# A four-layer convolution stack on one Trainium2 core: parts of g loaded three units ahead, and layer 1's last quarter spread over a longer stretch

## The chip, the cores and the metric

The kernel runs on one core of one Trainium2 chip. The metric is the device time of one execution in microseconds (us), as the median of several runs; lower is better. TensorE (PE) does the matmuls, VectorE (DVE), ScalarE (ACT) and GpSimd (POOL) do elementwise work, and SyncE's queue (SP) issues most of the DMA transfers. All five run their own queues of instructions and meet through semaphores.

## The reference

The input is `x` of shape (1024, 16, 16, 16), float32: 1024 images of 16 rows, 16 columns and 16 channels. Four layers are applied, each on a group norm of its input and with a residual:

```
def _gn(v, G=8, eps=1e-5):     # mean and variance of each image and group of 2 channels
    g = v.reshape(B_, H_, W_, G, C_ // G)
    return ((g - mean(g)) / sqrt(var(g) + eps)).reshape(v.shape)

x = x + L0(_gn(x), core0, core1, core2)          # a matrix of 4096 x 4096 in tensor-train form, ranks 1,16,16,1
x = x + L1(_gn(x), conv1, conv2, fc0, fc1)       # a step of a neural cellular automaton
x = x + L2(_gn(x), filters, bias)                # a 3x3 convolution over the image
x = x + L3(_gn(x), conv1, conv2, fc0, fc1)       # as L1, with its own weights
```

A step of the automaton (L1, L3) takes two depthwise 3x3 convolutions of its input, joins them with the input to 48 channels, applies `relu(flat @ fc0_w.T + fc0_b)` with 128 hidden values and `@ fc1_w.T + fc1_b`, adds the result `d` to its input, and sets to zero each place where the 3x3 maximum of channel 3 is not over 0.1, in the input or in `d`. Its reshapes read the channel axis as a place, so that the rows of the dense part come from all of an image; the kernel folds the convolutions into the weights of fc0.

## The kernel before

**Tiling.** The images are worked on in two half batches of 512, X0 and X1. Each stands in one large SBUF tile (`xn`, 128 partitions, 32 lines of 512 images). A line of a partition is one value of the 4096 of each image. The engines' queues are written out by the kernel itself: instructions stand on each engine in the order in which the Python code issues them.

**Layer 0.** The tensor-train matrix is multiplied in five phases, with products in the manner of Strassen (`PRODUCTS`), so that phases have 2, 7, 7, 7 and 7 products. Each phase has 16 *units* (a quarter `q` and a `w`), 80 in all. A unit needs its weights `w` (128 x 128 blocks), which are built on the chip: `gload(u)` (L1076) loads four parts of `g`, 32 KB each, from DRAM into a tile `gq`; `build(u)` multiplies them with the core `R` (`pw`, L1095, 16 matmuls in the first phase), and ScalarE copies the result to `w` (L1100). The parts of `g` are themselves products of the cores: `early` and `gs` multiply them (`pg`, L554), ScalarE copies them (L557), and `send` or `gs` store them to `g_dram` (L563, 512 KB each). A unit's matmuls `po` are at L1172. `pieces` issues them in steps of two: at the first step it builds the next unit's weights, at the second it stores the unit before (L1151 in the first phase), and in the middle of the unit (`at == mid`) it issues a later `gload`. In the first phase, TensorE also transposes the second half batch's input (`ptin`, L902), whose loads are issued on GpSimd's queue (L884).

**Layer 1.** `layer_nca` works in *quads*: four groups of rows of the hidden layer, each of several matmuls `ph` (L1562) into one of six PSUM banks (`h`), a ScalarE `Relu` to `hid` (L1565), and then L1398 into one of two banks `o`. Two quads make one step `w2`, and eight steps one quarter `q` of the output. In the first quarter the masks are made as well: at each step VectorE takes flags from the input (L1428) and from the result (L1406), adds bias and input (L1410), and some slots later TensorE counts the flags of the neighbours (`pcnt`, L1437, two of the `h` banks), from which VectorE makes the mask (L1442, L1443). GpSimd multiplies and adds (L1449, L1450), and SyncE stores.

**Work beside the matmuls.** `run(layer, us, loads, *spans)` places background work between the steps of a layer. Each span is a list of steps with costs and two fractions of the layer, for its begin and its end; a step is issued once the layer has passed its fraction. So the fractions set where in each engine's queue a background instruction stands, and no time is looked at when the kernel runs. Layer 1 on X0 begins before the group norm of X0 is complete: its last quarter of lines (24 to 31) is summed, centred and squared in the background (`last`: L614, L622, L655, L754, `pvar` L789), then come the root (L695), the Newton step (`newton`, L701 to L705: a reciprocal and four more), a spread over the partitions (`pr`, L801) with ScalarE's copy (L678), and four multiplications of two lines each (L655). The second quarter of the layer's steps is the first that reads these lines (`ph` with `wq`). The group norm of the other half batch, `norm_cw(X1)`, follows in the same manner.

Of the kernel before, what the change touches and what calls it, by code (L numbers as in the profile page):

```python
# [103 lines left out]
def conv_preact_kernel(ctx: ExitStack, tc: tile.TileContext, a: dict, out: bass.AP):  # L104
# [11 lines left out]
    xf = [  # L116
        [dram.tile([8, 4, P, NB], F32, tag=f"xf{l}_{n}", name=f"xf{l}_{n}") for n in range(NCH)]
        for l in range(5)
    ]
# [7 lines left out]
    def stage(es, sb, ps):  # L127

        for key, sizes, kw in (("sb", sb, {}), ("ps", ps, {"space": PSUM})):
            p = es.enter_context(  # L130
                tc.tile_pool(name=f"{key}{len(pool)}", bufs=1, reuse_waits="tile", **kw)
            )
            pool[key] = p, sizes
        pool[len(pool)] = None

    def work(shape, tag, name, dt=F32):
        p, sizes = pool["sb"]
        return p.tile(shape, dt, tag=tag, name=name, bufs=sizes[tag])
# [543 lines left out]
    def woven(steps, *more):  # L682

        out = []
        for i, step in enumerate(steps):
            out.append(step)
            out += [(0, x) if callable(x) else x for n, x in more if n == i + 1]
        return out
# [129 lines left out]
    def norm_cw(X, on_act):  # L818


        st, N = parts_cw(X, on_act)
        sums, sq, hold = N["sums"], N["sq"], N["held"]
        mean, var, keep, spread = N["mean"], N["var"], N["keep"], N["spread"]
        steps = sums[0] + woven(sums[1], (2, mean[0]), (3, hold[0])) + [1] + sq[0]
        for q in (1, 2):
            steps += woven(
                sums[q + 1], (2, var[q - 1]), (3, keep[q - 1]), (3, mean[q]), (4, hold[q])
            ) + [2] + sq[q][:4]
            if q == 1:
                steps += sq[q][4:]  # L830
        steps += woven(sq[2][4:], (2, mean[3]), (3, hold[3]))
        steps += woven(sq[3], (2, var[2]), (4, keep[2])) + [5, var[3], 2, keep[3]]
        return steps + rstd(st) + [4] + scaled(N, range(4))
# [18 lines left out]
    def load_cw(X, src):  # L852
        return [
            lambda q=q, w=w: nc.sync.dma_start(
                X[:, 8 * q + w : 8 * q + w + 2], src[w : w + 2, q].rearrange("w p b -> p w b")
            )
            for q in range(4)
            for w in range(0, 8, 2)
        ]
# [202 lines left out]
    def layer_train():  # L1062
# [7 lines left out]
        def gload(u):  # L1070
            if u >= len(units):
                return
            ph, q, w = units[u]
            st["g", u] = work([P, 2, P], "gq", "gq")
            for r in range(4):
                nc.sync.dma_start(  # L1076
                    st["g", u][32 * r : 32 * r + 32],
                    g_dram[phases[ph][0] // 2, w, :, :, 4 * q + r].rearrange("v k f -> k v f"),
                )
# [76 lines left out]
        def pieces(u, k):  # L1156

            ph, q, w = units[u]
            p, m0, m1 = phases[ph]
            matrix, what, goes = PRODUCTS[m0 + k]  # L1160

            late = 2 * (m1 - m0) - 1 if ph == 3 and q == w == 3 else 0
            mid = m1 - m0

            def go(t0):
                X, E = part_tile(p)
                if t0 == 0:
                    st["po"] = bank([P, NB], "o", "po0")
                po, at = st["po"], 2 * k + t0 // 2
                for t in range(t0, t0 + 2):  # L1170
                    x = E[:, what, t] if isinstance(what, int) else X[:, what[0], t, what[1]]
                    T.matmul(po, st["w", u][:, matrix, t], x, start=t == 0, stop=t == 3)  # L1172
                if at == 0:
                    build(u + 1)
                if at == 1 and u > 0:
                    store(u - 1)
                if at == mid:
                    gload(u + 2)

                for i in range(5):  # L1180
                    if at == min(5 + i, 2 * mid - 1):
                        mix(u + 1, i)
                if at == (late or mid):
                    fetch(u + 1)
                if at == 3 and ph in (2, 3):
                    residual(u)
                if t0 == 2:
                    gather(u, k, po, goes)
                if u == len(units) - 1 and at == 2 * mid - 1:
                    store(u)  # L1190

            return [lambda: go(0), lambda: go(2)]

        def gather(u, k, po, goes):
# [417 lines left out]
    X0, X1 = XN  # L1612
    gn = dict(t4=3, s=3, n=2)

    def steps_of(*more):
        return (lambda: None), [x for m in more for x in m]

    def now(steps):
        for step in steps:
            step = step[1] if isinstance(step, tuple) else step  # L1620
            if callable(step):
                step()
# [6 lines left out]
    L1, make1 = nca_weights("L1_conv_", X1[:, 0:16])  # L1629
    L3, make3 = nca_weights("L3_conv_", X1[:, 16:32])  # L1630
    with ExitStack() as es:
        stage(es, dict(gn, w=2, r=2, gq=2, R=1), dict(o=3, w=4, m=1))
        sums, cores, early, send, later = train_setup(XN[0].rearrange("p n b -> p (n b)")[:, 8192:14336])
        tag = ["w"]
        loads, stat, lines, tail, (spread0, spread1, kept) = input_steps(0, tag, nc.sync)
        now(loads)

        A.activation(work([P, NB], "n", "warm")[:, 0:1], ident[:, 0:1], AF.Sqrt)
        (gload, build, mixed, fetch), phases = layer_train()
        now([sums, cores] + stat[0] + stat[1] + lines[0][:4])  # L1640
        early(0)
        early(1)
        send(0, 0)
        gload(0)
        send(1, 0)
        gload(1)
        now(lines[0][4:8] + lines[1][:4] + tail[:2] + [spread0])
        send(0, 1)
        send(1, 1)
        build(0)  # L1650
        now(tail[2:] + [spread1, kept] + lines[0][8:10])
        fetch(0)
        now(normed(0, 0, 1, [(0, 0, 0), (0, 2, 0)]))
        mixed(0)
        now(normed(0, 0, 1, [(0, 0, 1), (0, 2, 1), (1, 0, 0), (1, 2, 0), (1, 0, 1), (1, 2, 1)]))
        now(combined(0, True))
        tag[0] = "mw"
        late = lines[0][10:] + lines[1][4:]
        loads, stat, lines, tail, more = input_steps(1, tag, G)
        tail += [(0, more[0]), 2, (0, more[1]), 2]  # L1660
        stat[1] = [[(2.6, s1[1]), s2] for s1, s2 in zip(stat[1][0::2], stat[1][1::2])]
        stat[0] = [[x] for x in stat[0]]
        woven_in = [
            x for j in range(2) for i in range(4) for x in stat[j][i] + lines[j][4 * i : 4 * i + 4]
        ]

        def mixed_in(xs, ys):

            n = len(xs)
            return [z for i, x in enumerate(xs) for z in (*ys[2 * i : 2 * i + 2], x)] + ys[2 * n :]  # L1670

        run(
            steps_of(phases[0]), 130, (),
            (late[:6] + mixed_in(loads[0:4], late[6:]) + mixed_in(loads[4:], later) + woven_in + tail + normed(0, 1) + combined(0, False), 0.0, 1.0),
        )
        run(
            steps_of(phases[1]), 350, (),
            (beside(make1, make3), 0.0, 0.74), (part_steps(1), 0.75, 0.98),
        )
        for i in (2, 3):  # L1680
            run(
                steps_of(phases[i]), 415, (), (part_steps(i), 0.05, 0.9),
                ([lambda: conv.update(s=conv_weights()), 60, lambda: conv["s"]()] if i == 2 else [0.0], 0.0, 0.5),
            )
        nst, N = parts_cw(X0, True, 3)
        for q in range(4):
            bg = alone(N, q - 1) if q else [0.0]
            if q == 3:
                bg = bg + rstd(nst, slice(0, 96)) + [3] + scaled(N, range(3))
            run(  # L1690
                steps_of(phases[4][56 * q : 56 * q + 56]), 104, [put(L1)] if q == 3 else (),
                (bg, 0.08, 0.95),
            )
    nst.clear()
    last = alone(N, 3) + rstd(nst, slice(96, 128)) + [3] + scaled(N, [3])
# [4 lines left out]
    with ExitStack() as es:  # L1700
        shared[0] = "o"
        stage(es, nca_sb, nca_ps)
        run(
            layer_nca(X0, 0, 1, L1), 250, load_cw(X1, xf[1][1]), (last, 0.0, 0.18),
            (norm_cw(X1, False), 0.21, 1.0), by=0.3,
        )
        run(
            layer_nca(X1, 1, 1, L1), 245, load_wc(X0, xf[2][0]), (norm_lines(X0, False), 0.2, 1.0), by=0.3
        )
# [48 lines left out]
```

## Time and profile before

| | us |
|---|---|
| runs | 3018.77, 3019.41, 3025.02 |
| median | 3019.41 |
| the profiled execution, its own time | 3020.7 |
| the profiled execution, span of its instructions | 3018.9 |
| TensorE busy | 2968.3 |
| VectorE busy | 1765.1 |
| ScalarE busy | 1102.6 |
| GpSimd busy | 669.5 |
| TensorE's granted clock, mean over the span | 0.991 |

The profile comes from one execution. Lines of a timeline give the start (us from the beginning of the span), the duration, the engine, the line of the kernel, the operation, what it writes and reads, and in brackets how long the engine had been idle before and what ended that. A table of windows gives for each stretch its length, the busy time and the number of instructions of PE, PEld (weight loads), DVE, ACT and POOL, then the granted clock (1.00 is full), the share of the 16 DMA engines that is busy, and GB/s. Ends of matmuls are modelled.

### The profile page before, as it was taken

The numbers are of one execution on the slowest core, as the hardware profiler recorded it, in microseconds if no ns is written. First come the engines' busy times: TensorE is split into PE (matmuls) and PEld (weight loads), VectorE is DVE, ScalarE is ACT, GpSimd is POOL, SyncE is SP. The second block draws the span as 40 slices with busy tenths as digits, with TensorE's granted clock in tenths as the row PEclk, the third lists the DMA queues.
The fourth block names the chain that finished last, engine by engine and source line by source line (L and its number), as shares of the span: only waits on it lengthen the run. The fifth ranks groups of instructions, "written<-read, shape, count | busy, mean of one in ns | idle before, by whom it ended". The sixth has DMA issues, their size and how long they took to land.

```text
span 3018.9 us, 36939 instructions
## 1 busy us (share of the span) xinstructions
PE 2968.3 (98%) x13876; PEld 1247.0 (41%) x13876; DVE 1765.1 (58%) x2352; ACT 1102.6 (37%) x1822; POOL 669.5 (22%) x727
## 2 busy tenths in 40 slices
PE   7999999999999999999999999999999999999997
PEld 5544334444444444444444433333333333333333
DVE  5354337555554555544555768856878766856433
ACT  4431441000000000000111146666667666666564
POOL 2035670200000000000000005434542323442321
PEclk8999999999999999999999999999999999999998
DMA  8643664533334433332222234445446866443466
GB/s 317 232 127 94 152 150 146 167 110 110 110 110 138 138 110 110 110 103 89 89 89 94 72 124 161 129 133 194 131 131 177 196 100 211 129 129 110 135 173 215
DMA packets 251523, 418.40 MB, mean 139 GB/s; under 512 B 34869, under 2 KB 105065, under 8 KB 248273
## 3 DMA queue, kind: packets, MB, share of 16 engines
q1 hardware_dynamic: 225776, 362.53, 36.6%
q0 software_dynamic: 25376, 53.38, 8.6%
q8 instruction: 110, 1.80, 0.3%
q14 instruction: 69, 0.56, 0.1%
q10 hardware_dynamic: 192, 0.13, 0.0%
HBM read 238.58 MB, written 165.53 MB: 134 GB/s over the span
## 4 chain that ended last, share of the span: by engine, by line
PE 90%; issue 2%; DVE 2%; DMA 2%; POOL 1%; ACT 1%; SPq 0%; POOLq 0%; DVEq 0%; ACTq 0%
PE po L1172 51%; PE ph L1562 21%; PE po L1398 8%; PE po L1260 3%; PE pw L1095 3%; PE L_conv_pe L392 1%; PE ptin L902 1%; PE po L1269 1%; DMA xn<-xf 1%; PE ptx L1460 1%; POOL res L1450 1%; POOL u L1449 1%; DVE sq L622 1%; PE pr L801 0%; DMA xn<-in_x_dram 0%
## 5 line engine op out<-in xcount | busy, mean ns | idle before, releaser
L1172 PE MATMUL po<-xn,w 128*128 128x512 f32 x3584 | 1577.4, 597 | 0.8 <-DVE xn L982 0.8
L1172 PEld LDWEIGHTS po<-xn,w 128*128 128x128 f32 x3584 | 671.7, 190 | 839.5 <-issue 820.9
L1565 ACT ACTIVATE hid<-ph,pack 128x512 f32<-128x512 f32 (+1 forms) x1040 | 655.6, 680 | 375.1 <-PE ph L1562 263.7
L1208 DVE TENSOR_TENSOR r<-r,po 128x512 f32<-128x512 f32 x576 | 378.2, 684 | 577.1 <-PE po L1172 524.7
L1449 POOL TENSOR_TENSOR u<-u,mask 128x512 f32<-128x512 f32 x123 | 193.8, 1576 | 1809.1 <-DVE mask L1443 1410.9
L1100 ACT COPY w<-pw 128x512 f32<-128x512 f32 (+1 forms) x320 | 150.6, 557 | 1209.6 <-issue 1006.4
L1562 PE MATMUL ph<-xn,wq 32*128 32x512 f32 (+1 forms) x3752 | 565.2, 599 | 0.0
L1562 PEld LDWEIGHTS ph<-xn,wq 32*128 32x128 f32 x3752 | 240.7, 184 | 263.9 <-issue 231.8
L1562 PE MATMUL ph<-xn,pack 32*128 32x512 f32 x1288 | 299.2, 625 | 4.6 <-DVE mask L1442 3.2
L1398 PE MATMUL po<-hid,pack 128*32 128x512 f32 (+1 forms) x2080 | 279.4, 600 | 0.0
L1113 DVE TENSOR_TENSOR w<-w 128x512 f32<-128x512 f32 x320 | 211.3, 687 | 86.6 <-ACT w L1100 86.6
L655 DVE TENSOR_TENSOR xn<-xn,m 128x1024 f32<-128x1024 f32 x160 | 216.3, 1383 | 35.5 <-ACT m L678 35.3
L1450 POOL TENSOR_TENSOR res<-res,u 128x512 f32<-128x512 f32 x123 | 204.5, 1663 | 9.6
L1410 DVE SCALAR_TENSOR_TENSOR u<-po,pack,xn 128x512 f32<-128x512 f32 (+1 forms) x130 | 96.3, 741 | 179.2 <-PE po L1398 175.1
L1260 PE MATMUL po<-xn,convw 128*128 128x512 f32 x368 | 163.9, 598 | 2.7 <-ACT conv L1310 2.7
L1562 PEld LDWEIGHTS ph<-xn,pack 32*128 32x128 f32 x1288 | 115.6, 186 | 105.2 <-issue 67.4
L1208 DVE TENSOR_TENSOR xn<-xn,po 128x512 f32<-128x512 f32 x96 | 64.4, 685 | 123.7 <-PE po L1172 123.3
L1398 PEld LDWEIGHTS po<-hid,pack 128*32 128x32 f32 x2080 | 42.8, 108 | 192.2 <-issue 134.3
L622 DVE TENSOR_TENSOR sq<-sq 128x1024 f32<-128x1024 f32 x75 | 106.2, 1416 | 11.1 <-ACT sq L640 10.4
L1260 PEld LDWEIGHTS po<-xn,convw 128*128 128x128 f32 x368 | 68.2, 190 | 97.8 <-issue 88.1
L404 POOL DMA_DIRECT2D L_conv_wy<-xn x160 | 88.8, 563 | 28.3 <-ACT xn L398 17.0
L1095 PE MATMUL pw<-R,gq 32*128 32x256 f32 (+1 forms) x1280 | 89.1, 384 | 1.0 <-DMA gq<-g_dram 1.0
(174 smaller groups left out, 1776.7 us busy)
## 6 DMA issues: line engine op xcount, KB each, us to landing
xf<-r SPq DMA_DIRECT2D x112, 512.0 KB, 3.8
xn<-xf SPq DMA_DIRECT2D x96, 512.0 KB, 4.7
r<-xf SPq DMA_DIRECT2D x80, 512.0 KB, 4.5
wq<-L_conv_wy SPq DMA_DIRECT2D x192, 192.0 KB, 2.7
res<-xf SPq DMA_DIRECT2D x128, 256.0 KB, 3.0
xf<-res SPq DMA_DIRECT2D x96, 256.0 KB, 2.0
res<-xr SPq DMA_DIRECT2D x256, 64.0 KB, 2.8
xf<-conv POOLq DMA_DIRECT2D x64, 256.0 KB, 5.9
```

Source lines behind the costliest of these rows:

```text
L655: V.tensor_tensor(part, part, m().unsqueeze(1).broadcast_to([P, 2, NB]), op)
L1095: T.matmul(pw[r][:, v], st["g", u][rows, v], st["R"][rows, p % 2, 64 * k0 : 256], start=True, stop=True,)
L1100: A.copy(w[:, k0:4, :, 32 * r : 32 * r + 32].rearrange("p k t (v o) -> p v (k t) o", v=2), pw[r],)
L1113: V.tensor_tensor(w[:, k], w[:, x], w[:, y], ALU.add if sign > 0 else ALU.subtract)
L1172: T.matmul(po, st["w", u][:, matrix, t], x, start=t == 0, stop=t == 3)
L1208: V.tensor_tensor(r[at], r[at], po, ALU.add if sign > 0 else ALU.subtract)
L1260: T.matmul(st["po", h][wh], conv["fw"][:, y], X[:, 16 * wh + h + y - 1], start=y == max(0, 1 - h), stop=y == min(2, S - h),)
L1398: T.matmul(po[32 * j : 32 * j + 32], nca["w1"][:, v], hid[j], start=v == 0, stop=v == 1)
L1449: by.tensor_tensor(u, u, st["m"][:, w2, cols(hf)], ALU.mult)
L1450: by.tensor_tensor(r, r, u, ALU.add)
L1562: T.matmul(ph, w, x, start=k == 0, stop=k == len(tiles) - 1)
L1565: A.activation(h, ph, AF.Relu, bias=nca["bt"][:, r : r + 1])
```

## The change

`gload` runs three units ahead instead of two, with a third buffer for `gq`, and the first three loads are issued before the first phase. The table of PSUM banks of this stage is written in another order. In layer 1 on X0, the background work on the last quarter is spread over the fractions 0 to 0.21 instead of 0 to 0.18, and the group norm of X1 starts at 0.23 instead of 0.21.

```
                 if at == mid:
-                    gload(u + 2)
+                    gload(u + 3)
...
-        stage(es, dict(gn, w=2, r=2, gq=2, R=1), dict(o=3, w=4, m=1))
+        stage(es, dict(gn, w=2, r=2, gq=3, R=1), dict(w=4, m=1, o=3))
...
         gload(0)
         send(1, 0)
         gload(1)
+        gload(2)
         now(lines[0][4:8] + lines[1][:4] + tail[:2] + [spread0])
         send(0, 1)
         send(1, 1)
...
         run(
-            layer_nca(X0, 0, 1, L1), 250, load_cw(X1, xf[1][1]), (last, 0.0, 0.18),
-            (norm_cw(X1, False), 0.21, 1.0), by=0.3,
+            layer_nca(X0, 0, 1, L1), 250, load_cw(X1, xf[1][1]), (last, 0.0, 0.21),
+            (norm_cw(X1, False), 0.23, 1.0), by=0.3,
         )
```

In the order of instructions that this gives, SyncE's queue has the four loads of `gload(2)` ahead of the stores of `send(0, 1)` and `send(1, 1)`, and every later `gload` serves the unit after. In layer 1, `pvar` stands behind the next `pcnt`, the Newton step stands behind the next L1428, L1442 and L1443, `pr` stands one `pcnt` later, the four multiplications L655 stand one step `w2` later, and the steps of `norm_cw(X1)` move on by one L1410. The numbers of matmuls and of elementwise instructions are the same.

More of the change, by code (lines that the diff above doesn't have):

```diff
@@ L1177, in go @@
                 if at == mid:
-                    gload(u + 2)
+                    gload(u + 3)
                 for i in range(5):
@@ L1631, in conv_preact_kernel @@
     with ExitStack() as es:
-        stage(es, dict(gn, w=2, r=2, gq=2, R=1), dict(o=3, w=4, m=1))
+        stage(es, dict(gn, w=2, r=2, gq=3, R=1), dict(w=4, m=1, o=3))
         sums, cores, early, send, later = train_setup(XN[0].rearrange("p n b -> p (n b)")[:, 8192:14336])
@@ L1646, in conv_preact_kernel @@
         gload(1)
+        gload(2)
         now(lines[0][4:8] + lines[1][:4] + tail[:2] + [spread0])
@@ L1703, in conv_preact_kernel @@
         run(
-            layer_nca(X0, 0, 1, L1), 250, load_cw(X1, xf[1][1]), (last, 0.0, 0.18),
-            (norm_cw(X1, False), 0.21, 1.0), by=0.3,
+            layer_nca(X0, 0, 1, L1), 250, load_cw(X1, xf[1][1]), (last, 0.0, 0.21),
+            (norm_cw(X1, False), 0.23, 1.0), by=0.3,
         )
```

## The prediction

> **What bounds the kernel now.** I read the page first: busy shares, the chain that ended last, and the row of the granted clock.
>
> ```profile
> PE 2968.3 (98%) x13876; PEld 1247.0 (41%) x13876; DVE 1765.1 (58%) x2352; ACT 1102.6 (37%) x1822; POOL 669.5 (22%) x727
> ...
> PEclk8999999999999999999999999999999999999998
> ...
> PE 90%; issue 2%; DVE 2%; DMA 2%; POOL 1%; ACT 1%; SPq 0%; POOLq 0%; DVEq 0%; ACTq 0%
> ```
>
> TensorE is busy 98% of the span and carries 90% of the chain, so only two things can shorten this kernel without removing matmuls: a gap in TensorE's stream, or time at a lower clock. Busy time does not show the second, because a matmul at half clock is busy twice as long. The list of TensorE's waits has only small sums (after the first 45 us at most 2.6 us at a time), so I looked in the timeline for each gap over 0.4 us and asked the stretches around it for the clock. Two places pay more than their gap. The first, TensorE in layer 0's first phase (start, duration, instruction, in brackets the idle time before it):
>
> ```profile
> 74.20 0.48 PE L1095 MATMUL pw<-R,gq 32*128 32x128 f32 x2
> 74.89 0.48 PE L1095 MATMUL pw<-R,gq 32*128 32x128 f32 x2 [0.21 <-DMA gq<-g_dram]
> 75.74 0.45 PE L1095 MATMUL pw<-R,gq 32*128 32x128 f32 x2 [0.36 <-DMA gq<-g_dram]
> 76.59 0.57 PE L1095 MATMUL pw<-R,gq 32*128 32x128 f32 x9 [0.40 <-DMA gq<-g_dram]
> ...
> 77.04 2.84 PE L554 MATMUL pg<-cores,xn 16*128 16x128 f32 x15
> 79.81 3.78 PE L1172 MATMUL po<-xn,w 128*128 128x512 f32 x4
> ```
>
> The 16 matmuls of one build take 74.20 to 77.04, 2.84 us, where the other builds of the phase take about 0.7 (63.82 to 64.48): each waits for one of the four parts of gq. Then four `po` matmuls take 3.78 us where later ones take 1.88. The windows say why (second last columns: granted clock, DMA share):
>
> ```profile
> 74.00:78.00 4.00, 3.01 (x24) 2.11 (x24) 0.00 (x0) 0.88 (x4) 2.56 (x5) 0.97 1.01 415
> 78.00:82.00 4.00, 3.91 (x14) 2.36 (x14) 3.31 (x9) 1.62 (x6) 0.00 (x0) 0.50 1.03 421
> ...
> 86.00:90.00 4.00, 4.00 (x14) 1.53 (x14) 0.00 (x0) 0.65 (x2) 0.00 (x0) 0.75 1.02 428
> 90.00:94.00 4.00, 3.51 (x22) 1.79 (x21) 0.00 (x0) 1.88 (x5) 0.00 (x0) 1.00 0.69 266
> ```
>
> The clock is at half from 77.79 to 88.03, 10.24 us. The second place is layer 1's first half batch, VectorE and then TensorE:
>
> ```profile
> 1793.58 0.75 DVE L1410 SCALAR_TENSOR_TENSOR u<-po,pack,xn 128x512 f32<-128x512 f32 x1
> 1794.36 3.35 DVE L701 RECIPROCAL r<-t 32x512 f32<-32x512 f32 x1
> ...
> 1799.64 0.69 DVE L705 TENSOR_TENSOR r<-r,t 32x512 f32<-32x512 f32 x1
> 1800.26 0.42 DVE L1428 TENSOR_SCALAR flags<-xn 32x512 bf16<-32x512 f32 x1
> 1800.70 0.69 DVE L1442 TENSOR_SCALAR mask<-pcnt 128x512 bf16<-128x512 f32 x1
> ```
> ```profile
> 1797.87 1.02 PE L1562 MATMUL ph<-nx,pack 32*128 32x512 f32 x2
> 1801.45 2.03 PE L1562 MATMUL ph<-xn,pack 32*128 32x512 f32 x2 [2.57 <-DVE mask L1442]
> 1803.41 1.94 PE L1398 MATMUL po<-hid,pack 128*32 128x512 f32 x8
> ```
>
> `pcnt` was complete at 1796.33, but its reader L1442 stood behind the five instructions of `newton` (L701 to L705, 1794.36 to 1800.33). `ph` needs that bank and waits 2.57 us; then the clock is at half from 1801.52 to 1808.35, 6.83 us.
>
> **What the skill says.** "TensorE: Matmul & The Clock Gate", Part 1, "What's actually happening": the array runs at half rate after an idle window of 3.413 us and at full rate after a busy one, and the windows run freely. The trace agrees: 10.24 and 6.83 us are three and two windows. It also shows that the window need not be wholly idle: the one before 77.79 held 15 `pw` and 6 `pg` matmuls. "PSUM — Partial Sum Buffer", "Engine vs sequencer instructions": VectorE's queue is strictly first in, first out; L1442 behind `newton` is that. "DMA: Bandwidth & Descriptors", "Issuing engines are not separate DMA queues": transfers from all queues share 16 engines. The trace agrees: in 60 to 80 us GpSimd's input loads hold them at 0.99, and gq's parts take 9.4 to 10.4 us to land, against 2.4 in the median.
>
> **The change, part by part.**
>
> *gq.* `gload(4)` is issued at 62.83 (the last of its four at 66.8), lands by about 76.5, and its build begins at 74.20. With three units ahead it takes the place of `gload(3)`, issued at 52.95: 21 us ahead of its build. So the build takes 0.7 instead of 2.84: **2.1 us**. `gload(5)` moves to 62.83 and lands by 76.5, its build is at 94.59 before and some 7 us earlier after: covered. No matmul is added. If the half clock goes too, half of 10.24, **5.1 us**, goes with it. As a check: this unit takes 20.39 us (74.20 to 94.59), the next 9.98; it has four more groups of eight `pg` at 0.65, 2.6, and one more 0.49 wait for a copy, 13.1 together; 7.3 us too much, against 2.1 + 5.1 = 7.2.
>
> What the two stretches are worth does not follow from each other. Between the build and `po` at 79.81 stand two groups of `pg` behind ScalarE's four copies of `pw` (1.20 us), so even without the wait for gq some 1.2 us of this stretch stay idle, and `pg` uses 16 of the 128 rows. With light and full windows both seen at full clock (98.27 to 101.69 with eight `pg`), and one of `pg` alone seen to end in half clock (19.77 to 23.18), I take the 5.1 at 60 in 100. Lower bound 0, upper 5.1.
>
> *The rest of this edit.* On SyncE's queue four issues (0.43 us median, 302 to 4467 ns) now stand ahead of the two 512 KB stores of `send(0, 1)` and `send(1, 1)`, and the first waits for `send(1, 0)` (issued 30.27, 6.7 us to landing): the stores slip from 35 to about 41 us. They are read first by `gload(8)`, issued in unit 5, after 94 us: covered by 50 us; no matmul or VectorE instruction waits for them. All later loads of g keep their place in the queue and only serve a later unit; the sum stays 320. The third buffer takes 1 KB per partition and moves `w` and `r` by as much. The other order of the bank sizes is read by name only, and every PSUM tile keeps its bank: **0**.
>
> *Layer 1's last quarter.* Its steps keep their number and move on by one or two slots. `newton` now stands behind the mask instructions that it blocked, and ahead of the next L1406. From the old durations: L1442 and L1443 1796.36 to 1797.85; `newton` (5.97) to 1803.85; L1406 to 1804.6. TensorE, without the 2.57 us wait, ends the unit's second L1398 at 1800.3, the next `ph` at 1802.2, L1398 at 1803.2, and reaches the last `pcnt`, which needs that L1406, at about 1803.6: a new wait of 1.0 us. Bounds 0.5 and 1.5 (one L1406 or L1410 earlier or later). Gain **1.6 us**, and **3.4** (half of 6.83) if the clock holds. A wait of 1.03 us on the same `pcnt` at 2544.40 was followed by one window at half clock, one of 1.20 at 2813.65 was not: I charge half of one window's loss, 0.5 × 1.7 = 0.85.
>
> The four multiplications L655 of the quarter end later. Measured from the L1443 that they follow, the first ends some 2 us before the first `ph` that reads its lines (1823.85 before), the second about 0.7 before its reader, the others more. The mask behind the last three comes 3.4 us after `pcnt` begins, when `ph` needs the bank: 0 to 0.6 us lost; 0.3 taken. `norm_cw` of the other half batch starts one L1410 later. VectorE is busy 17.1 of 20 us from 1840 to 1960, so it has room to catch up: 0; without that cover each L1410 behind one more L655 costs 1.2 us, for at most two or three of them.
>
> *Sum, both clocks held:* 2.1 + 5.1 + 1.6 + 3.4 − 0.85 − 0.3 = 11.0 us. The profiled execution took 3020.7 (span 3018.9), 1.3 above the median 3019.41 and inside the runs (3018.77 to 3025.02); I take the sum from the median: **3008.4**.
>
> **The rivals.**
>
> *One clock stays at half.* For it: both new stretches keep about 1 us of idle time, and the windows run freely. Against: both old ones had twice that. The gain is then 11.0 − 5.1 = 5.9 or 11.0 − 3.4 = 7.6: 3012 to 3013.5.
>
> *Neither clock gains.* Only the waits go, 2.1 + 1.6 − 0.3, and a window elsewhere may fall otherwise: 3016. Or the load ahead and the longer stretch do not bring what they say, for instance since a transfer that shares the saturated engines is still late: 3019.
>
> *Slower: the quarter comes too late.* The second half of the edit moves the last multiplications towards their readers. It decides when the first L655 ends more than 2 us later than I place it, because its factor passes TensorE, ScalarE and VectorE and each can hold it back by a `ph` group. Then TensorE waits in the three steps L1562 around 1824 to 1831, 1.5 to 3 us each, 4.5 to 9, with three to five windows at half clock, 5.1 to 8.5: 10 to 17 us lost. Less what gq gives (2.1 to 7.2) and with `newton`'s 5.0 not gained, the kernel takes 3022 to 3034; I take 3025. Against it: L655 has 2 us in hand and VectorE idles 1.0 to 3.9 us at a time around there.
>
> **How the numbers follow.** Both clocks held 0.44; one 0.28; waits alone 0.10; nothing 0.08; slower 0.10. 0.2%, about what a measurement of this kernel can tell from no change, is 6.0 us. Of the second case I count 0.23 as faster by more. Faster 0.67, within 0.22, slower 0.11 (a hundredth of "nothing" falls there). The range takes the gain's upper end (0.85 and 0.3 not lost, another light window held elsewhere, 3.4: 15.5, so 3004) and reaches over one clock and the waits alone to 3019.
>
> **What would show it.** After the change the build at 74 us takes 0.7 us with no wait for gq, and the clock stretches 74 to 98 us stay near 1.00; `po` then takes 1.9 us for four. In layer 1, RECIPROCAL stands behind L1443, the 2.57 us gap is gone, one of about 1 us stands ahead of `pcnt`, and no clock below 1.00 follows. I am wrong if the clock falls at these places though the waits are gone, or if `ph` waits for L655 at the first `wq` step.

## The result, and the profile after

The changed kernel takes **3012.03 us** (median of 11 runs, 3010.52 to 3013.44) against 3020.61 (11 runs, 3018.02 to 3025.02): a ratio of 0.9969, 95% interval 0.9961 to 0.9977, that is 8.6 us less. The profiled execution took 3013.1, its span is 3011.3, 7.6 less than the 3018.9 of before.

The page of the changed kernel: busy shares, granted clock, chain.

```profile
PE 2963.2 (98%) x13876; PEld 1242.9 (41%) x13876; DVE 1764.3 (59%) x2352; ACT 1102.9 (37%) x1822; POOL 668.1 (22%) x727
...
PEclk8999999999999999999999999999999999999998
...
PE 92%; DVE 3%; issue 2%; DMA 1%; ACT 1%; POOL 1%; SPq 0%; DVEq 0%; ACTq 0%; POOLq 0%
```

The same number of matmuls is busy 5.1 us less, with the same share of the span, and the page does not say why. The clock's record does for most of it: time at half clock fell by 6.83 us, worth 3.4 us of TensorE's work at the most. Another 1.4 is the build at 74 us, whose matmuls, issued in small groups between the waits, cover 2.10 us before and 0.73 now. The two places, first TensorE at the build that had waited for gq (timeline of the changed kernel):

```profile
73.96 0.73 PE L1095 MATMUL pw<-R,gq 32*128 32x128 f32 x16
74.51 1.33 PE L554 MATMUL pg<-cores,xn 16*128 16x128 f32 x8
76.23 0.72 PE L554 MATMUL pg<-cores,xn 16*128 16x128 f32 x8 [0.40 <-ACT g L557]
76.89 3.27 PE L1172 MATMUL po<-xn,w 128*128 128x512 f32 x4
```

The build takes 0.73 us and waits for no part of gq. But `po` again takes 3.27 us for four, and the windows of the changed kernel say why (granted clock third from last, then DMA share and GB/s):

```profile
74.00:78.00 4.00, 3.59 (x35) 2.57 (x35) 2.06 (x6) 2.40 (x8) 2.23 (x5) 0.93 1.00 415
78.00:82.00 4.00, 4.00 (x13) 1.70 (x12) 1.25 (x4) 1.23 (x3) 0.00 (x0) 0.64 1.02 418
82.00:86.00 4.00, 4.00 (x22) 1.84 (x21) 0.00 (x0) 0.98 (x3) 0.00 (x0) 1.00 1.03 426
...
323.00:330.00 7.00, 7.00 (x15) 1.99 (x15) 0.69 (x1) 4.25 (x8) 3.48 (x7) 0.51 0.50 154
1798.00:1802.00 4.00, 3.08 (x29) 0.80 (x22) 3.80 (x6) 3.25 (x6) 0.00 (x0) 1.00 0.85 253
1802.00:1808.00 6.00, 5.98 (x42) 2.48 (x42) 3.98 (x6) 3.21 (x5) 2.43 (x2) 1.00 0.19 72
2084.00:2088.00 4.00, 4.00 (x20) 1.32 (x24) 3.85 (x4) 1.94 (x4) 3.92 (x3) 0.57 0.19 55
```

Half clock comes in pieces of 3.41 us; such a piece is called a half-clock window below, while the rows of these tables are stretches that I chose. One half-clock window is left at 77.4 to 80.9, where there were three. At 1802 the clock holds. And the clock falls where it had not fallen before, at 323 and at 2084. Layer 1, VectorE and then TensorE of the changed kernel:

```profile
1794.48 0.69 DVE L1443 SCALAR_TENSOR_TENSOR mask<-pcnt,mask 128x512 bf16<-128x512 f32 x1
1795.21 3.35 DVE L701 RECIPROCAL r<-t 32x512 f32<-32x512 f32 x1
...
1800.49 0.69 DVE L705 TENSOR_TENSOR r<-r,t 32x512 f32<-32x512 f32 x1
1801.21 0.76 DVE L1406 TENSOR_SCALAR flags<-po,pack 32x512 bf16<-32x512 f32 x1
```
```profile
1800.27 0.82 PE L1437 MATMUL pcnt<-flags,alive_w 32*128 32x512 bf16 x5
1802.02 0.37 PE L1437 MATMUL pcnt<-flags,alive_w 32*128 32x512 bf16 x1 [0.94 <-DVE flags L1406]
1802.03 3.06 PE L1562 MATMUL ph<-xn,pack 32*128 32x512 f32 x16
```

`newton` now stands behind L1443, the 2.57 us gap is gone, and its new victim is L1406, for which `pcnt` waits 0.94.

To see where the time went I cut TensorE's stream of each profiled execution at the same instructions and took the length of each stage, with the time at half clock in it from the clock's record (in brackets). "Unit 4" is short for the time from the build of unit 4 at 74 us to the build of unit 5, "rest of layer 0" to the last L1172, "layer 1" to the first L1260, "conv" to the last L1260, "layer 3" to TensorE's last instruction; `before_again` and `after_again` are second profiles of the two kernels, the others are told below.

| profile | unit 4 | rest of layer 0 | layer 1 | conv | layer 3 |
|---|---|---|---|---|---|
| before | 20.39 (10.24) | 1661.66 (0) | 514.35 (6.83) | 208.16 (0) | 524.25 (3.41) |
| before_again | 20.39 (6.83) | 1663.76 (3.41) | 512.69 (3.41) | 210.26 (3.41) | 524.59 (3.41) |
| before_filled | 20.19 (3.41) | 1662.14 (0) | 513.49 (3.41) | 208.80 (0) | 523.40 (0) |
| gq_only | 13.74 (0) | 1664.84 (6.83) | 512.65 (3.41) | 210.84 (3.41) | 524.09 (3.41) |
| span_only | 19.08 (6.83) | 1662.39 (0) | 508.01 (0) | 209.86 (3.41) | 524.70 (3.41) |
| after | 15.37 (3.41) | 1664.74 (6.83) | 509.21 (3.41) | 208.86 (0) | 523.26 (0) |
| after_again | 19.12 (10.24) | 1661.46 (0) | 508.04 (0) | 208.39 (0) | 523.26 (0) |
| newton_split | 19.44 (10.24) | 1664.79 (6.83) | 508.03 (3.41) | 208.93 (0) | 523.24 (0) |
| both_filled | 14.40 (0) | 1661.46 (0) | 506.74 (0) | 210.78 (3.41) | 524.19 (3.41) |

From before to after: unit 4 −5.02, rest of layer 0 +3.08, layer 1 −5.14, conv +0.70, layer 3 −0.99, what lies ahead of unit 4 −0.23: together −7.6, the difference of the spans. The table lists nine of the thirteen profiles; the other four are those of `build_late`, `after_filled`, `all_filled` and `both_late`.

### The profile page after: what moved, and what is told of

Read it like the earlier page. It is cut to its first block, busy times and chain, and to the rows that moved or that the text cites. A ratio compares the mean times of both kernels' runs of the same rounds, so it can differ in the third digit from the quotient of the medians.

```text
span 3011.3 us, 36933 instructions
## 1 busy us (share of the span) xinstructions
PE 2963.2 (98%) x13876; PEld 1242.9 (41%) x13876; DVE 1764.3 (59%) x2352; ACT 1102.9 (37%) x1822; POOL 668.1 (22%) x727
## 4 chain that ended last, share of the span: by engine, by line
PE 92%; DVE 3%; issue 2%; DMA 1%; ACT 1%; POOL 1%; SPq 0%; DVEq 0%; ACTq 0%; POOLq 0%
PE po L1172 52%; PE ph L1562 22%; PE po L1398 8%; PE po L1260 3%; PE pw L1095 3%; PE ptin L902 1%; PE L_conv_pe L392 1%; DVE bn L896 1%; PE po L1269 1%; PE ptx L1460 1%; DVE sq L622 1%; PE pr L801 0%; DVE xn L655 0%; ACT hx L1248 0%; POOL res L1450 0%
## 5 line engine op out<-in xcount | busy, mean ns | idle before, releaser
L1172 PE MATMUL po<-xn,w 128*128 128x512 f32 x3584 | 1577.6, 597 | 0.7 <-DVE xn L982 0.7
L1172 PEld LDWEIGHTS po<-xn,w 128*128 128x128 f32 x3584 | 671.2, 190 | 840.6 <-issue 820.2
L655 DVE TENSOR_TENSOR xn<-xn,m 128x1024 f32<-128x1024 f32 x160 | 214.9, 1375 | 37.2 <-ACT m L678 37.0
L1410 DVE SCALAR_TENSOR_TENSOR u<-po,pack,xn 128x512 f32<-128x512 f32 (+1 forms) x130 | 96.2, 740 | 181.1 <-PE po L1398 175.0
L1260 PE MATMUL po<-xn,convw 128*128 128x512 f32 x368 | 164.0, 598 | 3.2 <-ACT conv L1310 3.2
L1260 PEld LDWEIGHTS po<-xn,convw 128*128 128x128 f32 x368 | 68.2, 190 | 98.5 <-issue 88.2
L622 DVE TENSOR_TENSOR s<-s,xn 128x1024 f32<-128x1024 f32 x60 | 87.5, 1458 | 2.4 <-DMA xn<-xf 0.6
```

The source lines that it names most:

```text
L622: V.tensor_tensor(st["t"], st["t"], x, ALU.add)
L655: V.tensor_tensor(part, part, m().unsqueeze(1).broadcast_to([P, 2, NB]), op)
L1260: T.matmul(st["po", h][wh], conv["fw"][:, y], X[:, 16 * wh + h + y - 1], start=y == max(0, 1 - h), stop=y == min(2, S - h),)
```

## The experiments

**The two parts alone.** `gq_only` is the first part of the diff without the other order of the table of banks, which no run tries alone; `span_only` is the second part:

```diff
-    gload(u + 2)            ->  gload(u + 3), gq=2 -> gq=3, one more gload(2)      # gq_only
-    (last, 0.0, 0.18), (norm_cw(X1, False), 0.21, 1.0)
+    (last, 0.0, 0.21), (norm_cw(X1, False), 0.23, 1.0)                             # span_only
```

> Only the first part of the change: three buffers, loads three units ahead; layer 1's spans as before. Theory (each part brings its wait and the half clock that followed it, and the parts add): the build at 74 us takes 0.7 us, unit 4 takes 15.4 us instead of 20.4 with one half-clock window left; layer 1 keeps the 2.57 us gap and its half clock; 4 to 6 us less than before. Rival (the lead of layer 0 is lost again before layer 1, as the profile of the changed kernel lets one suspect: 5.4 us at 200 us, 2.2 at 1757): 1 to 3 us less.

> Only the second part: layer 1's last quarter over 0.21, the other half batch from 0.23; two buffers of g and loads two units ahead. Theory: RECIPROCAL stands behind L1443, the gap of 2.57 us goes and one of 0.9 us stands ahead of pcnt; without the two half-clock windows 1801 to 1808: 3 to 5 us less than before. With the first part's own gain the sum is the 8.6 of the whole change. Rival (the whole gain comes from layer 0): under 1.5 us.

Measured: `gq_only` 3017.45 us against 3021.17, ratio 0.9991 (0.9982 to 0.9999); `span_only` 3014.33, ratio 0.9977 (0.9968 to 0.9986). `gq_only` gained a little less than the 4 to 6 us expected, 3.7, and its interval only just leaves out no change; `span_only` gained more than the 3 to 5, 6.8. The product of the two ratios, 0.9968, is close to the whole change's 0.9969, so they may well add. By the medians the larger part is the one in layer 1, though the intervals overlap. In its profile layer 1 is 6.3 us shorter than before, without half clock; another 1.3 comes from unit 4, which this edit does not touch and where the load of g that ends the unit (see below) landed earlier. In `gq_only` the clock held in unit 4 (its windows):

```profile
74.00:78.00 4.00, 3.59 (x32) 2.22 (x24) 2.49 (x7) 2.40 (x8) 1.81 (x4) 1.00 1.02 421
78.00:82.00 4.00, 4.00 (x23) 2.03 (x22) 0.83 (x3) 1.55 (x5) 0.00 (x0) 1.00 1.02 412
82.00:86.00 4.00, 3.51 (x22) 1.84 (x21) 0.00 (x0) 2.10 (x7) 0.00 (x0) 1.00 1.01 422
```

The busy time in the first of these, 3.59 of 4.00, is that of the changed kernel to the hundredth, where the clock fell. So unit 4 took 13.74 us, and the expectation of one half-clock window left was wrong for this execution; then the clock fell at 320 and 392 us, 3.3 us of the 6.6 won. So half of the lead is lost again before layer 1, which comes near the rival, but to half clock and not to a wait. The DMA engines were as full here (share 1.01 to 1.02) as where the clock fell, so their traffic alone does not bring half clock.

**The same kernels again.** No edit.

> The kernel before, profiled a second time. Theory: build at 74 us again with about 2 us of waits for gq, 2.57 us ahead of ph; some half clock after both (their light stretches are long enough for most offsets), of one to three windows; elsewhere it may differ (320, 2545). Rival: the same windows at the same places as in the first profile.

> The changed kernel, unchanged, profiled a second time. Theory (the clock's windows start at another point of the kernel in each execution, and only a light stretch that falls inside one window costs): the gaps and waits are the same to 0.1 us, but the half-clock windows lie partly elsewhere than at 77, 323 and 2084 us; the edges of the windows have another offset. Rival (the half clock belongs to the place): the same four windows again at the same places.

`after_again` (3011.5 us) has the waits of `after` and other half clock: three windows in unit 4, none at 323, none at 2084 (windows of that profile):

```profile
74.00:78.00 4.00, 2.93 (x29) 2.32 (x22) 2.48 (x7) 2.12 (x8) 2.09 (x4) 0.78 1.01 419
78.00:82.00 4.00, 4.00 (x10) 1.46 (x11) 0.83 (x3) 0.92 (x3) 0.00 (x0) 0.50 1.03 424
82.00:86.00 4.00, 4.00 (x10) 1.46 (x8) 0.00 (x0) 0.68 (x3) 0.00 (x0) 0.50 1.01 420
...
323.00:330.00 7.00, 6.30 (x36) 1.93 (x29) 1.38 (x2) 6.08 (x12) 1.79 (x4) 1.00 0.74 244
2084.00:2088.00 4.00, 4.00 (x31) 1.53 (x35) 3.85 (x4) 2.42 (x4) 3.90 (x3) 1.00 0.32 111
```

So half clock does not belong to a place. Nor were the waits in unit 4 quite the same: the gap ahead of the second `pg` was 1.06 us here and 0.40 in `after`. `before_again` (3022.99) gave the more important line. Its unit 4 has two half-clock windows instead of three and is as long to a hundredth, because its end waits (timeline of that profile, the next build):

```profile
90.44 1.98 PE L1172 MATMUL po<-xn,w 128*128 128x512 f32 x4
94.10 1.16 PE L1095 MATMUL pw<-R,gq 32*128 32x128 f32 x14 [1.67 <-DMA gq<-g_dram]
```

**The waits left, the clock held.** `before_filled` puts matmuls of 128 rows that nobody reads into the idle time of both waits:

```diff
+        def busy(u, n):          # u == 4: n matmuls ident x R, 128x256, into a free bank of po
...
                     T.matmul(pw[r][:, v], st["g", u][rows, v], ...)
+                    if v == 0 and r < 3:
+                        busy(u, 1)
+            busy(u, 1)
...
+    # ahead of the last ph of the step that stalls in layer 1: five matmuls ident x X[:, 0], 128x256
```

> The kernel before, both waits left as they are, with added matmuls (128 rows, 128x256, about 0.47 us each, their result never read) in the idle time of the two waits: four in the build at 74 us, five ahead of the stalled ph at 1801. Theory (the half clock follows from too little work of TensorE in the window before it, whatever the wait): the build still takes 2.1 us more than the other ones and the stalled ph still starts about 2.5 us after its predecessor ended, but the clock stays at 1.00 at both places: 5.1 + 3.4 less, 0 to 0.5 of added time, so 8 us less than before. Rival (half clock comes with the wait itself or with the traffic of the DMA, not with idle TensorE): 0 to 1 us more than before, half clock as before.

Measured: 3019.2 us against 3021.17, ratio 0.9994 (0.9986 to 1.0003): nearly nothing of the 8 us. Both theories of the expectation fail at one point each. In layer 1 the clock did hold (timeline of TensorE, then windows of `before_filled` and, last, of the kernel before for the same stretch):

```profile
1797.45 2.43 PE L1545 MATMUL po<-xn,ident 128*128 128x256 f32 x10
1800.09 1.12 PE L1581 MATMUL ph<-xn,pack 32*128 32x512 f32 x2 [0.21 <-DVE mask L1455]
...
1804.34 0.66 PE L801 MATMUL pr<-r,sel 32*128 32x512 f32 x1 [1.07 <-DVE u L1423]
```
```profile
1800.00:1808.00 8.00, 6.84 (x44) 1.97 (x44) 2.65 (x5) 3.25 (x6) 2.42 (x2) 1.00 0.45 159
```
```profile
1800.00:1808.00 8.00, 6.55 (x23) 1.88 (x26) 3.99 (x7) 1.77 (x3) 2.42 (x2) 0.60 0.29 88
```

The trace counts the five added matmuls as ten. `ph` still waits for the mask, the matmuls ahead of it end at 1799.88, and the clock is 1.00 instead of 0.60; the four profiles with this wait and no added matmuls all have one or two half-clock windows here. So it is TensorE's light work that lets the clock fall, not the wait. But TensorE at full clock then ran into a wait of 1.07 us ahead of `pr`, which the half clock had hidden. In layer 0 the two windows that went gave nothing at all (timeline of `before_filled`):

```profile
75.68 0.71 PE L1105 MATMUL pw<-R,gq 32*128 32x128 f32 x10
...
89.36 1.98 PE L1185 MATMUL po<-xn,w 128*128 128x512 f32 x4
92.74 1.33 PE L1105 MATMUL pw<-R,gq 32*128 32x128 f32 x16 [1.39 <-DMA gq<-g_dram]
```

The added matmuls filled the first wait, and the build of unit 5 waits 1.39 us for its own g. The first part of that load is issued at 80.5 us here and at 81.5 before, and lands some 12 us later, at 92.7 and 94.1.

**One build a step later.** That gave a new theory: with loads two units ahead the end of unit 4 is set by the landing of `gload(5)`. In the first profile this does not show as a wait, since TensorE, at half clock, reached the next build just when g landed (parts at 94.1 to 94.7):

```profile
94.59 0.93 PE L1095 MATMUL pw<-R,gq 32*128 32x128 f32 x16
```

```diff
-                if at == 0:
+                if at == (1 if u == 3 else 0):
                     build(u + 1)
```

> The kernel before (two buffers, loads two units ahead) with only this build moved: the build of the unit whose g lands at 76 us is issued one po step later (about 2.5 us), when its g is there. Theory formed from the runs so far (what sets the end of this unit is the landing of the next unit's g, issued at 80 to 81.5 us and there at 92.5 to 94.6, whatever the wait and the clock before it): the wait of 2.1 us at this build is gone, but the next build still begins at 92.5 to 94.6; time as before, 0 to 1 us less. Rival (the prediction's step: the wait at this build is what costs): the next build begins 2 us earlier, and more if the clock holds; 2 to 5 us less.

Measured: 3023.68 us against 3021.98, ratio 1.0007 (0.9999 to 1.0015). The timeline of this kernel:

```profile
76.60 0.72 PE L554 MATMUL pg<-cores,xn 16*128 16x128 f32 x8 [1.75 <-ACT g L557]
...
80.50 1.03 PE L1095 MATMUL pw<-R,gq 32*128 32x128 f32 x16
...
92.62 1.07 PE L1095 MATMUL pw<-R,gq 32*128 32x128 f32 x4 [1.69 <-DMA gq<-g_dram]
94.32 1.06 PE L1095 MATMUL pw<-R,gq 32*128 32x128 f32 x12 [0.62 <-DMA gq<-g_dram]
```

The wait for g at the first build is gone, though 1.75 us of waiting for ScalarE's copy stand ahead of `pg` now. The next build begins at 92.62, 2 us earlier than before, which fits the rival as well; but TensorE was free from 90.9, waited 2.3 us for g in two pieces, and the build ends at 95.4, where it ended before (95.5). So the theory holds, and the rival's 2 to 5 us are not there. What the first part of the change does in layer 0 is therefore not to remove the wait that one sees at 74 us; it removes a bound at 92 to 94 us that the wait and the half clock together had just filled. Issuing the load somewhat earlier would not lift this bound: in all thirteen profiles the load issued at 78 to 82 us lands no earlier than 91.3.

**The changed kernel with the light stretch filled.**

```diff
                         start=True, stop=True,
                     )
+            busy(u, 2)
             for r in range(4):
                 A.copy(w[:, k0:4, ...
```

> The changed kernel with two such added matmuls (0.94 us) between the build at 74 us and the pg groups. Theory (the one half-clock window left there, 77.4 to 80.9, comes of the light stretch of pw and pg with 0.4 us idle): the window is gone, 1.7 us less, against 0.5 to 0.9 of added time: 0.8 to 1.2 us less than the changed kernel. Rival (16-row pg matmuls draw too little in any case, or the window falls by chance): half clock stays, 0.5 to 0.9 us more.

3009.11 us (3007.07 to 3010.99), ratio 0.9959 (0.9947 to 0.9972): 2.9 less than the changed kernel's median instead of the 0.8 to 1.2 expected; the two were measured at different times and the intervals of their ratios overlap, but of the five runs only the slowest, 3010.99, is above the changed kernel's fastest, 3010.52. Unit 4 took 14.40 with no half clock, 0.66 more than the 13.74 without the added matmuls. I had counted the one window of the first profile; `after_again` shows that it can be three.

> The changed kernel with added matmuls, their result never read, in five light stretches: two of 128x256 after the build at 74 us, four of 128x128 ahead of the third group of L_conv_pe (gap of 0.70 at 320 us), and one of 128x256 inside the gap ahead of the last pcnt in layer 1 (both half batches, 0.94 and 0.42 us) and layer 3's first (1.03). Theory: no half-clock window in layers 0, 1 and 3 in any execution, so about 3006 us, and runs that differ less than those of the changed kernel; the added matmuls cost 1 to 1.5 us in all. Rival (half clock falls by chance whatever TensorE does): 3012 to 3014, with windows as before.

```diff
+    # besides the edit of after_filled:
+    # ahead of the third L_conv_pe group: four matmuls ident x ident, 128x128
+    # ahead of the pcnt that waits, at three places: one matmul ident x X[:, 0], 128x256
```

3010.33 us (3007.64 to 3011.88). The profile has full clock from 30.9 to 2990 us, as the theory says, but the time is not below that of `after_filled`, whose profile has full clock from 40.6 us on, too. Against that profile layer 1 is 0.7 us longer here and layer 3 is 1.2 longer. The cost was mis-sized: the matmul added ahead of `pcnt` writes a bank of `po` that VectorE had not read yet, and made a longer wait than the one that it was to fill (timeline of `all_filled`; it was 0.94):

```profile
1794.01 0.81 PE L1458 MATMUL pcnt<-flags,alive_w 32*128 32x512 bf16 x5
...
1796.63 0.67 PE L1457 MATMUL po<-xn,ident 128*128 128x256 f32 x2 [1.81 <-DVE u L1428]
```

The runs differ no less (4.2 us), and their mean clocks tell in part why: 0.997 in the two at 3007.6 and 3007.8, 0.994 in the three at 3010.3 to 3011.9. So more half clock did fall in the slower ones; where, only a profile would show.

**Newton in five steps.**

```diff
-        return [2, root, 3, (6, newton)]
+        return [2, root, 3, (3.4, one)] + [(0.65, one)] * 4     # layer 1's last quarter: one instruction each
```

> The changed kernel with the five instructions of newton of layer 1's last quarter as five steps instead of one, so that VectorE's mask and residual instructions can come between. Theory (the 0.94 us wait ahead of pcnt is L1406 behind 6 us of newton): the gap falls to 0 to 0.4 us; 0.5 to 0.9 us less in layer 1, which is not to be told from no change by the time alone (3011.2 to 3012). Rival (the wait only moves): the same gap at the next mask, or pr waits for the last of newton, up to 1 us.

3011.13 us (3008.09 to 3015.89), ratio 0.9968 (0.9956 to 0.998). VectorE of this kernel:

```profile
1799.09 3.35 DVE L701 RECIPROCAL r<-t 32x512 f32<-32x512 f32 x1
1802.47 0.76 DVE L1414 TENSOR_SCALAR flags<-po,pack 32x512 bf16<-32x512 f32 x1
1803.26 0.75 DVE L1418 SCALAR_TENSOR_TENSOR u<-po,pack,xn 128x512 f32<-128x512 f32 x1
1804.02 0.42 DVE L1436 TENSOR_SCALAR flags<-xn 32x512 bf16<-32x512 f32 x1
1804.37 0.68 DVE L702 TENSOR_TENSOR t<-r 32x512 f32<-32x512 f32 x1
```

The flags (here L1414) go right behind RECIPROCAL, `pcnt` no longer waits, and no gap over 0.4 us appears at `pr` or the next mask: the stretch from the last L1172 to the first `ph` that reads `wq` takes 58.73 us instead of 60.05. The other profiles agree: 58.75 in both kernels below that split `newton`, 60.03 to 60.05 in `span_only`, `after_again` and `after_filled`, all at full clock there. A gain of 1.3 us, more than the 0.5 to 0.9 expected, that the time alone could not have told.

**Both, in two ways.** `both_late` is the changed kernel with `newton` split and the build of unit 4 one step later (the edit of `build_late`), `both_filled` with `newton` split and the two matmuls of `after_filled`.

> The changed kernel with newton in five steps and with that same build one po step later, so that the pw matmuls and the two groups of pg no longer stand in one light stretch. Theory: without half clock the span is 3004.4 - 1.3 = 3003; the unit loses 0 to 1 windows instead of the 1 to 3 that the two profiles of the changed kernel show; other places (320, 2084, conv) fall by chance as before: 3007 to 3010, 2 to 4 us less than the changed kernel. Rival (the place of the build doesn't matter to the clock): 3010.7, newton's 1.3 alone.

> The changed kernel with newton in five steps and the two added matmuls after the build at 74 us. Theory: the two gains add, since one lies in layer 0 and the other in layer 1: 1.3 less than the 3009.1 of the added matmuls alone, 3007.8. Rival: 3009 and more, since the light stretch that no longer falls at one place falls at another.

`both_late`: 3008.91 us (3008.53 to 3016.07), ratio 0.9966 (0.9953 to 0.9978). The median is in the expected band, but the profiled execution (3016.07) is the counterexample to its theory: five half-clock windows, 77.3 to 94.3, after a gap of 2.82 us between two groups of `pg`, 0.40 in the changed kernel (its timeline):

```profile
73.83 0.72 PE L554 MATMUL pg<-cores,xn 16*128 16x128 f32 x8
...
74.16 0.72 POOL L925 DMA_DIRECT2D xr<-lines  x1 [2.94 <-ACT lines L923]
...
76.94 0.65 ACT L557 COPY g<-pg 128x256 f32<-128x256 f32 x2 [3.09 <-DMA xr<-lines]
...
77.37 1.23 PE L554 MATMUL pg<-cores,xn 16*128 16x128 f32 x8 [2.82 <-ACT g L557]
```

ScalarE's copy L557 waits for a transfer out of `lines`: `g` and `lines` take turns in the three buffers of `t4`, and the DMA engines are full there (share 1.00 to 1.03 in the windows above). This is what is late next in unit 4, once g of the unit is early or its build out of the way: the 1.75 us in `build_late` are the same wait. A fourth buffer for it was not tried. The other runs fit their clocks: 3008.5 to 3008.9 us in the three with a mean clock of 0.995 or more, 3013.5 in the one with 0.993, 3016.1 in the profiled one with 0.991.

`both_filled`: **3008.09 us** (3005.65 to 3009.46), ratio 0.9954 (0.9941 to 0.9968), 0.3 off the 3007.8 expected; the rival's "3009 and more" is not excluded by five runs. It has the lowest median here, and its slowest run is below the changed kernel's fastest, 3010.52; from `after_filled` and `both_late` the runs do not tell it apart.

## Why the prediction was right or wrong

The measured 3012.03 lies 3.6 us above the predicted 3008.4, inside the range, on the faster side, and where the rival "one clock stays at half" put it (3012 to 3013.5). The agreement with that rival's number is in part luck. Of the 3.6, 1.2 is the kernel before, whose median is 3020.61 over all its runs and was 3019.41 over the three that I had; the gain is 8.6 for 11.0. And in the profiled pair the terms were others than the rival's: unit 4 brought 5.0 where the sum had 7.2, layer 1 brought 5.1 where it had 3.85, and 2.6 were lost at places that the sum does not name. Step by step:

- **The build no longer waits for gq.** Right: 0.73 us, and `gload(5)` was covered as argued.
- **2.1 + 5.1 in unit 4.** This is the step that failed. The check, 7.3 us too much against 7.2, was a coincidence of two bounds of equal length: 7.2 us of waiting and half clock, and a load that landed just then. Without half clock the unit takes 13.74 us after the change (the count gave 13.1), so 6.6 could be won at best; but before the change little of the 5.1 could be had from the clock alone: 20.39, 20.39 and 20.19 us with three, two and one half-clock windows. With loads two units ahead the unit lasted until `gload(5)` landed; in `span_only`, where that was at 92.5 us, it took 19.08 with two. I had looked up when `gload(5)` lands after the change, not what it bounded before. What is won depends on the windows that remain: 6.6 with none, 5.0 with one, 1.0 to 1.3 with three, and the profiles show each. "60 in 100" for a held clock looks too high: of the four profiles with early g and nothing else changed in this unit (`gq_only`, `after`, `after_again`, `newton_split`) one held.
- **1.2 us of idle time behind the pw copies.** Partly right: the copies account for 0.40; the rest, up to 1.06 in `after_again` and 2.82 in `both_late`, is the wait of L557 for `t4`, which I did not list. In the kernel before, the wait for gq covered it: with that wait gone, `build_late` waits 1.75 there.
- **Newton.** Right: 2.57 us gone, a new wait of 0.94 for the 1.0 predicted, at the `pcnt` named. Without half clock layer 1 goes from an estimated 510.9 (514.35 less half of 6.83; no profile shows it) to 508.0 (`span_only`, `after_again`): 2.9 us, not 1.6 − 0.3. A gap of 0.59 us at 1821, `ph` behind another mask, went too, and the 0.3 for a mask behind L655 was not seen; the rest of the difference I cannot place.
- **3.4 for the clock in layer 1, less 0.85.** Right in sign: the old gap cost one or two windows in every profile that has it unfilled (by the half clock alone an estimated 1.7 to 3.4 us), and the new gap none in any of the four that have it; the 0.85 was not due.
- **L655.** The first one ended 0.8 us before its reader (1813.29 against 1814.12), not 2; the rival "slower" was nearer than I put it, but `ph` waited for no L655.
- **Half clock elsewhere.** The prediction had it only in the range's 3.4 and, without a size, in the rival "neither clock gains". In the profiled pair it took back 3.1 at 323 us and 1.2 at 2084 and gave 1.0 at 2545.

## What to carry to other kernels

A stall that one removes is worth what the next bound of that stretch leaves: look for the transfer or the wait that lands just after it, above all where half clock has been hiding it, and test by holding the clock with matmuls that nobody reads. When the result depends on where a light stretch falls, one profile of each kernel is one draw; compare several, stage by stage, with the time at half clock beside each. A long VectorE block in a background job can be cut into single instructions as well as moved: here that took away the wait that moving it had left, 1.3 us.

## What the runs showed that I had not expected

**Whether a light stretch is followed by half clock goes with its offset in a fixed grid.** The Trainium skill ("TensorE: Matmul & The Clock Gate", Part 1, "What's actually happening") speaks of windows of 3.413 us that run freely. In each profile here all changes of the clock, up to the last work, lie on one grid of that step to 0.01 us, with another offset in each execution. I took the begin of a gap that nearly every profile has, 1.03 us ahead of `pcnt` in layer 3, and its offset from the edge of its window. In the kernel before it begins at 2544.40, the window ends at 2545.63, so the offset is 3.41 − 1.23 = 2.18; in the changed kernel it is 2.76. Here are the gap and the clock after it, before:

```profile
2545.43 0.84 PE L1437 MATMUL pcnt<-flags,alive_w 32*128 32x512 bf16 x2 [1.03 <-DVE mask L1442]
```
```profile
2544.00:2550.00 6.00, 4.97 (x26) 1.76 (x27) 4.49 (x6) 1.57 (x3) 3.66 (x3) 0.72 0.35 111
```

and after:

```profile
2538.83 0.59 PE L1437 MATMUL pcnt<-flags,alive_w 32*128 32x512 bf16 x2 [1.03 <-DVE mask L1442]
```
```profile
2537.00:2543.00 6.00, 4.64 (x34) 1.55 (x35) 4.88 (x7) 2.34 (x5) 3.27 (x2) 1.00 0.43 134
```

Over the twelve profiles that have this gap, the six offsets from 1.09 to 2.29 us were all followed by a window at half clock, the six from 2.36 to 3.11 by none. The gap of 0.70 at 320 us sorts as cleanly: half clock at 0.34, 1.18 and 1.35, none at 0.02 and from 1.46 up. Even the gap of 0.42 us at 2082, among bf16 `pcnt` matmuls, was followed by half clock at 1.38 to 1.96 and not elsewhere (up to 0.17, and from 2.68). So a gap of 0.42 us may cost 1.2 (layer 1 of `after` against `after_again`), and the 2.11 us gap ahead of L1260 in the conv stage nothing when an edge of the grid cuts it in two (offsets 2.20 to 2.98, eight profiles).

No idle window is needed for it: in the 3.41 us ahead of each fall of the clock between 45 and 2980 us, in the thirteen profiles, the trace counts TensorE as busy for 0.7 to 3.15 us. The most, 3.15, is at 392 us in `gq_only` (388.6 to 392.0), nearly all of it `pw` matmuls of 32 rows and `L_conv_pe` matmuls of 9.

**A half-clock window costs one to two us, or nothing.** Layer 3 with one is 1.0 longer than without (524.25 against 523.26), the rest of layer 0 with two is 3.3 longer (1664.74 against 1661.46), conv with one is 1.8 longer on the average (four profiles against five of the table); unit 4 with loads two ahead gained 0.2 from losing two.
